# Mask chunks every three steps and more pieces of list work per step in layer 0's last dense blocks

## The chip, the core and the metric

The kernel runs on one core of a Trainium2 chip, with five engines that run side by side: PE (TensorE, matrix products), DVE (VectorE), ACT (ScalarE), POOL (GpSimd, here mostly issuing gathers) and SP (SyncE, issuing the other DMAs). The metric is the device time of one execution in microseconds, as the median of several runs; lower is better.

## What is computed

Four graph attention layers stand one behind the other over 4096 nodes with 256 features, all with one adjacency matrix. Layer 0, on which the change acts, is:

```python
h = jnp.maximum(_layernorm(x, axis=-1), 0.0)
h = h @ W.T + b_W
e = (h @ a1)[:, None] + (h @ a2)[None, :] + b_a[0]
e = jnp.where(e > 0, e, 0.2 * e)
scores = jnp.where(adjacency_matrix > 0, e, jnp.float32(NEG_INF))
attention = jax.nn.softmax(scores, axis=1)
x = x + attention @ h
```

Layers 1 to 3 have the same form with other heads and ends (layer 2 four heads, layer 3 a positive and a negative softmax). Adjacency is sparse and uneven: node i and node j are joined with a chance that falls with both numbers, so the first nodes have many neighbours and the last ones few.

## The kernel before

**Tiles.** Nodes lie in 32 tiles of 128, and eight blocks of four tiles. A target tile is done in one of two ways. Dense: the layer's first blocks (`DENSE = (4, 2, 1, 1)`, so blocks 0 to 3 in layer 0) go over all 32 source tiles, one step each; a step makes a 128x512 matrix of weights on DVE (`weigh`, L1151) and multiplies it on PE into four sums (L1193). Listed: for a target tile T of a later block, the few sources that any of its nodes have are gathered by POOL from a table in DRAM (`gather`, L532) with an index list of T, and a listed tile has 5 to 8 steps in layer 0. Four tile columns are weighed from `mpre` without a gather, then "single" gathers (s_gg), then "quad" ones of four gathers each (s_gq).

**Masks.** The adjacency matrix is loaded by SP in chunks of four source tiles by one block, in two halves (`load`, s_raw, four buffers). `mask_chunk(ib, c)` turns such a chunk into bytes on DVE (two conversions, L1472), writes it to DRAM for later layers, and notes in `seen[ib]` which sources occur (L1483). Each call also issues the next chunk's load. Dense block ib makes its own chunks as it goes, one every `CH = 4` steps; the chunks of blocks 4 to 7 are made at `sides`, one every third step, from step 2 to step 95 of the 128 dense steps. So none are left for block 3, which is steps 96 to 127.

**Lists.** When a block's eighth chunk is done, a generator `list_sources` waits for its turn (`TURNS = (4, 5, 6, 1, 7, 2, 3)`) in the queue `lists_q`. It makes the index lists of four tiles in pieces: counts (L882 to L889), a first placing (pre_p, tot_p, two matmuls, a scan L869 and an addition L878), a second placing (pre_s, tot_s, and the cast to lof), values (L928), and then per tile two one-hots of 128x1792 on DVE (L943), 28 matmuls on PE (L968, idx_ps) and the copy into an index tile (L978). A piece may give a pause in an estimated clock.

**Order.** `run(plan)` goes through the plan, which interleaves dense steps and listed steps: from dense step 48 on, one or two listed steps stand behind every dense one. At a position of the plan it fetches (makes masks, issues gathers), begins (ACT copies of gathered masks), weighs three positions later and multiplies six positions later. After each multiplied step it draws pieces from two queues: `pump(posts, rates[0])` (normalization and projection of finished tiles for layer 1, `node_rows`, with transposes s_tp, copies s_hT and products s_pj) and `pump(lists_q, rates[1])`; then up to `rates[2]` gathers of masks. A fetch that needs an index that is not there draws pieces by force. After the plan's last step what is left is drawn by force too:

```python
run(plan + listed)
push(lists_q, find_flag())
while lists_q:
    pump(lists_q, 1, force=True)
    pump(posts, 1, force=True)
```

Only then layer 1 is recorded. A scheduler puts the instructions on the engines by this order, with some freedom; POOL keeps the written order. On one engine instructions run in their order, so a waiting instruction holds all behind it. PSUM, into which PE writes, is split in six buffers for sums (`s_acc`) and two (`ps_mm`, tag "mm") that serve everything else: s_tp, s_pj, s_sT (target rows, emptied by ACT as s_grow, L1042), pre, tot and idx_ps.

Blocks 1, 2, 3 keep masks beside the rows of a layer's table. Block 7's masks (tiles 28 to 31) lie with layer 0's rows in `table_own`: a gather brings the mask too, and ACT copies it to `mlist` (L1174 for a single gather, L1084 for a quad). In layer 0 its gathers need the index of tile 28, the fifth list to be made.

Of the kernel before, what the change touches and what calls it, by code (L numbers as in the profile page):

```python
# [21 lines left out]
NT = N // P  # L22
IB = 512
NIB = N // IB
IT = IB // P
CH = 4
NCH = NT // CH
# [432 lines left out]
DENSE = (4, 2, 1, 1)  # L460
# [29 lines left out]
def list_layers(ctx: ExitStack, tc: tile.TileContext, a: dict, out: bass.AP, flag):  # L490
# [65 lines left out]
    def table_rows(t, jt):  # L556

        r0 = jt // CH * CH * P
        r0 += 1 if r0 >= HALF else 0
        return t[r0 : r0 + CH * P, :].rearrange("(p k) d -> p k d", k=CH)  # L560
# [4 lines left out]
    def mask_rows(b, jt):  # L565
        if b not in MASKS_IN:
            return table_rows(mask_t[b], jt)
        l, behind = MASKS_IN[b]
        c0 = FRONT[l] + GW[l] if behind else 0
        return table_rows(table[l], jt)[:, :, c0 : c0 + MW].bitcast(U8)  # L570
# [6 lines left out]
    def weights(l, pool, prep, q):  # L577


        L = layers[l] = Layer()  # L580
        L.l = l
        L.H, L.part = LH[l], PART[l]

        ncols = D + 3 * L.H + (D if l == 3 else 0)
        L.w = pool.tile([P, 2, ncols], F32, name=f"s_w{l}", tag=f"s_w{l}")
        L.s = small.tile([P, NT, L.H], F32, name=f"s_s{l}", tag=f"s_s{l % 2}", bufs=1)
        L.ready = [False] * NT
        L.bias = None
        L.table = table[l]
        L.made = False  # L590
        L.making = make_weights(L, pool, prep, q)
        return L
# [97 lines left out]
    def push(queue, work, delay=0.0):  # L690
        queue.append([work, clock[0] + delay])
# [14 lines left out]
    def ensure(done):  # L706
        while not done():
            assert posts
            pump(posts, 1, force=True)
# [141 lines left out]
    def list_sources(ib, seen, pool, consts):  # L851
# [75 lines left out]
        for k, block in enumerate(blocks_of):  # L927
            nc.vector.scalar_tensor_tensor(  # L928
                val[:, k, :],
                hib,  # L930
                float(block),
                code.rearrange("p t j -> p (t j)"),
                op0=ALU.is_equal,
                op1=ALU.mult,
            )
            if k % 4 == 3:
                yield
# [456 lines left out]
    with ExitStack() as phase:  # L1394
# [28 lines left out]
        L0 = weights(0, prep, prep, nc.scalar)  # L1423
# [19 lines left out]
        def load():  # L1443

            n = len(loaded)
            if n == len(order):
                return
            ib, c = order[n]
            loaded[order[n]] = []
            for h in range(2):  # L1450
                raw = stage.tile([P, half, IB], I32, name=f"s_raw_{ib}_{c}_{h}", tag="raw")
                r0 = (c * CH + h * half) * P
                nc.sync.dma_start(
                    raw,
                    a["adjT"][r0 : r0 + half * P, ib * IB : (ib + 1) * IB].rearrange(
                        "(c p) i -> p c i", p=P
                    ),
                )
                loaded[ib, c].append(raw)

        def mask_chunk(ib, c):

            load()
            if ib == 0:
                behind(c)
            m = (
                mpre[:, :, ib * IB : (ib + 1) * IB]
                if c == 0
                else mpool.tile([P, CH, IB], U8, name=f"s_m_{ib}_{c}", tag="m")
            )  # L1470
            for h, raw in enumerate(loaded[ib, c]):
                nc.vector.tensor_scalar(m[:, h * half : (h + 1) * half, :], raw, 0.0, None, op0=ALU.is_gt)  # L1472
            if ib == OWN0:
                rows_at = table_rows(table_own, c * CH)
                nc.sync.dma_start(rows_at[:, :, 0:HW].bitcast(U8), m[:, :, 0 : IB // 2])
                nc.sync.dma_start(rows_at[:, :, HW + GW[0] :].bitcast(U8), m[:, :, IB // 2 :])
            elif c > 0 or ib in MASKS_IN:
                nc.sync.dma_start(mask_rows(ib, c * CH), m)
            if ib > 0:
                if c == 0:  # L1480
                    seen[ib] = lists_p.tile([P, IT * GR, JT], BF16, name=f"seen_{ib}", tag="seen", bufs=4)
                else:
                    nc.vector.tensor_reduce(  # L1483
                        seen[ib][:, :, (c - 1) * CH : c * CH].rearrange("p a j -> p j a"),
                        m.rearrange("p j i -> p (j i)")
                        .bitcast(I32)
                        .rearrange("p (j a w) -> p j a w", j=CH, w=GP // 4),
                        AX.X,
                        ALU.max,
                    )  # L1490
                if c == NCH - 1:
                    waiting[ib] = list_sources(ib, seen[ib], lists_p, consts)
                    while turns and turns[0] in waiting:
                        push(lists_q, waiting.pop(turns.pop(0)))
            return m

        def behind(c):

            if c + 4 < NIB:
                load_x(c + 4)  # L1500
            if c == 4:
                zero_rows()
            if c == 5:
                L1 = weights(1, const, prep, nc.sync)
                L1.pre = keep.tile([P, DP, GW[1]], F32, name="pre1")
                L1.rows = rows_of(L1, rows)
                L1.pool = rows
                next(L1.making)
                push(posts, L1.making, 15.0)

        def block(ib):
            masks = {}

            def get(jt):
                if jt % CH == 0:
                    masks[jt // CH] = mask_chunk(ib, jt // CH)
                for k, at in enumerate(sides):
                    if at == ib * NT + jt:
                        mask_chunk(DENSE[0] + k // NCH, k % NCH)
                c = ib * NT + jt - sides[-1] - 1  # L1520
                if 0 <= c < NCH:
                    nc.sync.dma_start(
                        table_rows(table_own, c * CH)[:, :, HW : HW + GW[0]], L0.g[:, c * CH : (c + 1) * CH, :]
                    )
                ensure(lambda: L0.ready[jt])
                return [0], [L0.g[:, jt, :]], masks[jt // CH][:, jt % CH, :]

            return Unit(L0, ib * IT, IT, NT, get, big="growb", rates=(2, 2, 1))

        load_x(0)  # L1530
        load()
# [6 lines left out]
        for T in range(DENSE[0] * IT, NT):  # L1538
# [7 lines left out]
                rates=(1, 2, 0),  # L1546
# [3 lines left out]
        for ib in range(DENSE[0]):  # L1550
            for step in block(ib).plan():
                plan.append(step)
                if ib * NT + step[1] >= LISTED0:
                    n = 1 + step[1] % 2
                    plan += listed[:n]
                    del listed[:n]
# [23 lines left out]
    for l in (1, 2, 3):  # L1580
# [41 lines left out]
        else:  # L1622
            per = L.H
            first = []
            for ib in range(DENSE[l]):
# [6 lines left out]
                    big="o" if ib else "growb",  # L1632
                    cost=0.9 if l == 2 else 1.7,
                    per=per,
                    rates=(2, 0, 0),
# [84 lines left out]
```

## Time and profile before

| | us |
|---|---|
| median of 3 runs | 1544.14 |
| lowest, highest | 1542.4, 1545.57 |
| profiled execution, device time | 1640.54 |
| its span, first to last instruction | 1638.8 |

The profiled execution is 6% longer than a run without the profiler; all times of single instructions are of it. Its engines over the span:

```
PE 1445.7 (88%) x10558; PEld 1084.8 (66%) x10558; DVE 1182.5 (72%) x3424; ACT 497.3 (30%) x1569; POOL 1037.6 (63%) x1255
```

PEld is the load of weights into PE, beside the products. Layer 0's dense block 3 begins at about 345 us, its last dense product ends at 489.5 us, and layer 1's first transposes are at 519.2 us. "[4.60 <- X]" behind an instruction says that its engine was idle for 4.60 us before it and that X ended that.

### The profile page before, as it was taken

The page shows a single profiled execution, that of the slowest core. Times are in us where ns is not written, and L with a number is a line of the kernel's source. Part 1 is how long each engine was busy: PE and PEld are TensorE (multiplying, and loading weights), DVE is VectorE, ACT ScalarE, POOL GpSimd, SP SyncE. Part 2 cuts the span into 40 slices and gives each one's busy share as a digit, 9 for nine tenths or more (in the row PEclk, how much of TensorE's full clock was granted, in tenths as well). Part 3 has the DMA queues.
Part 4 walks back from the last instruction along what each step waited for, and adds up shares of the span by engine and source line. Part 5 has one row for each costly group of instructions (what it writes and reads, how often), then busy time and mean ns, then how long its engine had stood idle before and what let it go on. Part 6 is the DMA issues. An engine that isn't in the chain of part 4 may idle for free.

```text
span 1638.8 us, 30153 instructions
## 1 busy us (share of the span) xinstructions
PE 1445.7 (88%) x10558; PEld 1084.8 (66%) x10558; DVE 1182.5 (72%) x3424; ACT 497.3 (30%) x1569; POOL 1037.6 (63%) x1255
## 2 busy tenths in 40 slices
PE   6999898888888988888989889987877999899995
PEld 4887676666676866666645545566655877688873
DVE  6889989887677467655778879876755466577754
ACT  5631020011112023222335545565744111111111
POOL 9825888883513477767337776555556277867775
PEclk9999999999897999998999999989877999999997
DMA  7899999876414454554323333333333477766665
GB/s 261 283 320 297 320 299 293 223 201 161 115 33 145 112 152 126 141 154 133 114 73 107 97 105 97 106 90 99 91 102 106 131 217 209 217 193 198 205 184 146
DMA packets 161024, 272.72 MB, mean 166 GB/s; under 512 B 29664, under 2 KB 86462, under 8 KB 160862
## 3 DMA queue, kind: packets, MB, share of 16 engines
q1 hardware_dynamic: 117322, 146.32, 28.6%
q0 software_dynamic: 42704, 123.84, 28.2%
q8 instruction: 86, 1.41, 0.4%
q14 instruction: 76, 0.62, 0.1%
q10 hardware_dynamic: 836, 0.53, 0.1%
HBM read 225.22 MB, written 45.39 MB: 165 GB/s over the span
## 4 chain that ended last, share of the span: by engine, by line
PE 49%; DVE 7%; issue 6%; POOL 4%; DMA 4%; ACT 2%; another core or an unknown queue 1%; DVEq 0%; POOLq 0%; ACTq 0%
PE s_acc L1193 26%; PE s_pj L778 6%; PE s_acch L1210 5%; PE s_accm L1228 5%; DVE s_p L1151 3%; POOL s_gq L532 3%; PE s_acc L1130 2%; PE s_sT L1036 2%; DMA s_gq<-table,idx 1%; DMA s_gg<-table,idx 1%; PE s_acch L1130 1%; PE s_tp L746 1%; POOL s_gg L532 1%; DVE s_p L1160 1%
## 5 line engine op out<-in xcount | busy, mean ns | idle before, releaser
L532 POOL DMA_INDIRECT s_gq<-table,idx x400 | 431.8, 1080 | 188.7 <-issue 83.2
L532 POOL DMA_INDIRECT s_gg<-table,idx x258 | 277.2, 1074 | 277.4 <-DVE first L943 55.2
L1193 PE MATMUL s_acc<-g,s_p 128*128 128x257 f32 x1152 | 294.4, 401 | 17.4 <-DVE s_p L1151 12.2
L1193 PEld LDWEIGHTS s_acc<-g,s_p 128*128 128x128 f32 x1152 | 221.0, 200 | 59.7 <-DVE s_p L1151 16.5
L1193 PE MATMUL s_acc<-s_gs,s_p 128*128 128x257 f32 x896 | 212.3, 388 | 1.1 <-issue 0.9
L1151 DVE SCALAR_TENSOR_TENSOR s_p<-s_grow,pre,mpre 128x128 f32<-128x128 f32 (+1 forms) x576 | 188.4, 367 | 28.8 <-PE s_acc L1193 16.3
L778 PE MATMUL s_pj<-s_w,s_hT 128*128 128x259 f32 (+3 forms) x640 | 184.9, 428 | 24.4 <-issue 9.8
L1151 DVE SCALAR_TENSOR_TENSOR s_p<-s_grow,s_gs,s_ms 128x512 f32<-128x512 f32 x224 | 159.6, 748 | 56.5 <-PE s_acc L1193 20.1
L1193 PEld LDWEIGHTS s_acc<-s_gs,s_p 128*128 128x128 f32 x896 | 166.5, 192 | 39.0 <-issue 7.6
L1193 PE MATMUL s_acc<-pre,s_p 128*128 128x257 f32 x768 | 186.3, 391 | 3.2 <-issue 2.2
L1193 PEld LDWEIGHTS s_acc<-pre,s_p 128*128 128x128 f32 x768 | 147.2, 196 | 28.9 <-issue 4.3
L778 PEld LDWEIGHTS s_pj<-s_w,s_hT 128*128 128x128 f32 x640 | 126.2, 208 | 57.8 <-issue 14.4
L1193 PE MATMUL s_acc<-s_gg,s_p 128*128 128x257 f32 x530 | 137.9, 392 | 6.9 <-DVE s_p L1151 3.5
L1151 DVE SCALAR_TENSOR_TENSOR s_p<-s_grow,s_gg,mlist 128x128 f32<-128x128 f32 x363 | 116.5, 344 | 33.6 <-PE s_acc L1193 22.5
L541 POOL MEMSET pause<- 128x256 f32 x379 | 132.3, 349 | 0.2
L532 POOL DMA_INDIRECT mlist<-mask_t,idx x77 | 91.1, 1183 | 65.2 <-DVE idx L978 46.4
L1042 ACT ACTIVATE s_grow<-s_sT 128x256 f32<-128x256 f32 (+2 forms) x136 | 46.9, 368 | 257.4 <-PE s_sT L1036 136.5
L1107 DVE TENSOR_TENSOR s_p<-s_grow,s_gq 128x128 f32<-128x128 f32 (+1 forms) x168 | 52.4, 339 | 97.5 <-DMA s_gq<-table,idx 53.7
L1193 PEld LDWEIGHTS s_acc<-s_gg,s_p 128*128 128x128 f32 x530 | 100.2, 194 | 29.9 <-issue 8.5
L1210 PE MATMUL s_acch<-pre,s_p 128*64 128x65 f32 x1792 | 92.8, 237 | 28.9 <-issue 26.6
L1210 PEld LDWEIGHTS s_acch<-pre,s_p 128*64 128x64 f32 x1792 | 72.3, 144 | 67.0 <-issue 39.3
L1090 ACT ACTIVATE s_p<-s_grow,s_minus,pre 128x128 f32<-128x128 f32 x224 | 96.0, 485 | 62.0 <-PE s_accm L1228 25.7
(154 smaller groups left out, 2077.9 us busy)
## 6 DMA issues: line engine op xcount, KB each, us to landing
s_raw<-in_adjT SPq DMA_DIRECT2D x128, 512.0 KB
s_gs<-table SPq DMA_DIRECT2D x28, 516.0 KB
table<-s_g SPq DMA_DIRECT2D x28, 258.0 KB
mask_t<-s_m SPq DMA_DIRECT2D x28, 256.0 KB
s_ms<-mask_t SPq DMA_DIRECT2D x28, 256.0 KB
s_gq<-table,idx POOLq DMA_INDIRECT x400
table<-s_m SPq DMA_DIRECT2D x21, 256.0 KB
table<-g SPq DMA_DIRECT2D x8, 516.0 KB
```

The costliest lines, as they stand in the source:

```text
L532: nc.gpsimd.indirect_dma_start(out=dst, out_offset=None, in_=src, in_offset=bass.IndirectOffsetOnAxis(ap=index_ap, axis=0), element_offset ...
L541: nc.gpsimd.memset(pause, 0.0)
L778: nc.tensor.matmul(ps, lhsT=hT[:, c, :], rhs=L.w[:, c, k * (D + 6) : k * (D + 6) + cols], start=(c == 0), stop=(c == 1),)
L1036: nc.tensor.transpose(ps[:, h - h0, it, :], L.s[:, T0 + it, h : h + 1].to_broadcast([P, P]), ident)
L1042: nc.scalar.activation(grow[:, h1:h2, :], ps[:, h1 - h0 : h2 - h0].rearrange("p h a b -> p h (a b)"), AF.Exp, scale=scale,)
L1090: nc.scalar.activation(w[:, h, :], u.grow[:, h, :], AF.Relu, scale=g[h][:, n - 1 : n], bias=minus)
L1107: nc.vector.tensor_tensor(p4[:, h0:h1], grow[:, h0:h1], c[:, h0:h1].to_broadcast([P, h1 - h0, GR, GP]), op=op)
L1130: nc.tensor.matmul(acc, lhsT=p[:, h, part], rhs=g[:, k, h * n : (h + 1) * n - 1], start=False, stop=last, skip_group_check=True,)
L1151: nc.vector.scalar_tensor_tensor(p[:, k, :], u.grow[:, h, :], g[k][:, n - 1 : n], m, op0=ALU.min if L.l == 3 and h == 1 else ALU.max, op1= ...
L1193: nc.tensor.matmul(u.accs[it][h], lhsT=p[:, k, it * P : (it + 1) * P], rhs=g[k][:, 0:n], start=first, stop=last, skip_group_check=u.quads > 0,
L1210: nc.tensor.matmul(u.accs[0][c : c + P // 2, h, :], lhsT=p[:, h, c : c + P // 2], rhs=g[h][:, 0 : DH + 1], start=first and h == 0, stop=la ...
L1228: nc.tensor.matmul(u.accs[h], lhsT=g[k][:, 0 : DH + 1], rhs=p[:, k, :], start=first, stop=last, skip_group_check=True,)
```

## The change

In dense block 3 a chunk is made every three steps, at steps 0, 3, ..., 21, instead of every four, at steps 0, 4, ..., 28. In block 2 three pieces of list work are drawn after a dense step, and in block 3 four, instead of two; blocks 0 and 1 and the listed steps in between keep two. What is computed stays as it was.

```diff
         def block(ib):
             masks = {}
+            every = CH if ib < DENSE[0] - 1 else CH - 1
 
             def get(jt):
-                if jt % CH == 0:
-                    masks[jt // CH] = mask_chunk(ib, jt // CH)
+                if jt % every == 0 and jt // every < NCH:
+                    masks[jt // every] = mask_chunk(ib, jt // every)
...
-            return Unit(L0, ib * IT, IT, NT, get, big="growb", rates=(2, 2, 1))
+            return Unit(L0, ib * IT, IT, NT, get, big="growb", rates=(2, max(2, ib + 1), 1))
```

## The prediction

> **What bounds the kernel now.** I read in this order: the slices of the page (where PE, the matrix engine, has gaps), the table by stages for the 300 us around the change, the sums of waits there, and then PE, ACT and DVE instruction by instruction. First the stages (columns: stretch in us, its length, then busy us and count of PE, weight loads, DVE, ACT, POOL, then the granted PE clock, DMA share, GB/s).
>
> ```profile
> 240.00:345.00 105.00, 89.00 (x501) 69.35 (x499) 90.87 (x233) 14.27 (x52) 89.69 (x99) 0.97 0.92 252
> 345.00:385.00 40.00, 33.84 (x220) 26.52 (x219) 28.98 (x82) 6.64 (x24) 33.54 (x41) 0.92 0.65 160
> 385.00:414.00 29.00, 28.50 (x155) 22.92 (x156) 27.37 (x76) 4.54 (x17) 1.72 (x2) 0.94 0.61 159
> 414.00:441.90 27.90, 25.89 (x174) 21.42 (x174) 16.19 (x38) 5.13 (x19) 22.83 (x27) 0.88 0.47 117
> 441.90:461.70 19.80, 11.10 (x52) 8.38 (x50) 14.48 (x40) 2.39 (x9) 6.53 (x7) 0.89 0.40 111
> 461.70:489.40 27.70, 27.70 (x177) 23.28 (x177) 21.65 (x64) 2.53 (x10) 0.00 (x0) 0.95 0.06 20
> 489.40:519.20 29.80, 22.83 (x204) 17.66 (x202) 23.65 (x75) 9.39 (x34) 4.70 (x6) 0.71 0.38 116
> ```
>
> To 345 us POOL, DVE and DMA are all near 90%; dense block 3 then runs to 489.4 us and is held by PE, except at 441.9 to 461.7, where PE works 11.1 of 19.8 us. The last row is the drain: no dense step is left, and the rest of the lists (2 and 3) is forced out before layer 1 may begin. The two holes at 442 and 457, from the sums of waits and then from ACT and PE in order of time:
>
> ```profile
> PE tot_p L866 <- ACT s_grow L1042: 4.6, 1, 4.6
> PE pre_s L864 <- ACT s_hT L748: 4.1, 1, 4.1
> ```
> ```profile
> 446.00 0.30 ACT L1084 COPY mlist<-s_gq 128x128 uint8<-128x128 uint8 x1 [7.27 <-DMA s_gq<-table_own,idx]
> 446.21 0.27 ACT L1042 ACTIVATE s_grow<-s_sT 128x128 f32<-128x128 f32 x1
> ...
> 460.72 0.30 ACT L1084 COPY mlist<-s_gq 128x128 uint8<-128x128 uint8 x1 [4.53 <-DMA s_gq<-table_own,idx]
> 460.93 0.64 ACT L748 COPY s_hT<-s_tp 128x256 f32<-128x256 f32 x2
> ```
>
> List 2's tot_p needs one of the two ps_mm buffers; it is held by s_sT of tile 30; ACT empties it, but only behind a copy that waits for a gather from table_own. The hole at 457 is the same with s_hT and tile 31's gather. So one late gather stops PE through ACT's queue and a PSUM buffer. The drain, on DVE:
>
> ```profile
> 501.08 1.12 DVE L869 TENSOR_TENSOR_SCAN off_p<-going,tot_p 128x464 f32<-128x464 f16 x1 [2.32 <-PE tot_p L866]
> ...
> 507.42 1.08 DVE L943 TENSOR_TENSOR first<-place,lof 128x1792 f16<-128x1792 f16 x1
> 508.42 1.57 DVE L928 SCALAR_TENSOR_TENSOR val<-hib,code 128x112 f16<-128x112 f16 x8
> 509.90 2.29 DVE L943 TENSOR_TENSOR first<-place,lof 128x1792 f16<-128x1792 f16 x2
> ```
>
> From the scan at 501.08 to layer 1's first transpose at 519.22 it is one chain, list 3's own, with eight one-hots of 1.08 us at its end.
>
> **What the Trainium skill says.** "TensorE: Matmul & The Clock Gate", Architectural detail: ACT and DVE queues are strict FIFO, only PE pulls weight loads ahead; the trace agrees (s_grow ran 0.21 us after the copy that it did not need). The same page, Part 1, gives half clock to an idle PE; here the drain was granted 0.59 at 500 to 510 and 0.50 at 510 to 520 us. "Perfetto Trace Analysis", Optimizing Tensor Performance, wants matmul groups to rotate through PSUM banks so that evacuation overlaps; with two ps_mm buffers, shared by lists, transposes, projections and target rows, the 4.6 and 4.1 us show what two are worth when ACT is blocked.
>
> **The change, part by part.** The scheduler settles the order, so I counted pieces as the program is built and compared the built order on each engine.
>
> Rates. Block 2 pumps three pieces a step and block 3 four, instead of two. When the last step is recorded, 11 pieces of list 2 and 43 of list 3 are left before, and 0 and 40 after. On PE, 49 index matmuls of list 2 (of 161) leave the drain; on DVE two one-hots and the last index copies. POOL's order is identical, and from layer 1 on PE's too.
>
> (a) Drain. Before: 489.5 us (487.57 + 1.98, last dense matmul) to 519.2 = 29.7 us. After, pre_p stands on PE right behind the two transposes of tile 30/31, instead of behind those, list 2's 49 matmuls and the projections of 30, 31, 12, 13. The scan becomes DVE's limit: normalization of tiles 30/31 and the ends of 12 to 15 (about 5 us at the pitches of the before rows), scan and add 1.7, list 3 to shared with the statistics of 12 to 15 between 4.7, second placing to lof 3.0, one-hots and val 10.3 (507.42 to 517.73), last matmuls and flag 1.5: 26 us. The path gains about 4 (8 if DVE runs ahead over the first part; 0 if two PSUM buffers string it out). The projections of 14 and 15 now stand between index matmuls, so layer 1's gathers start later relative to layer 1; its first listed weight is some 28 us after its start, which covers that. −4.
>
> (b) The same 49 matmuls now stand between dense steps 25 to 30, where PE is 100% busy (27.70 of 27.70): at 0.80 us per 14 they cost 2.8. The two one-hots lie on DVE, which has 6 us free there: 0; without that cover 2.2. +2.8.
>
> (c) The two holes. Index 28, which starts the gathers of tiles 28 to 31, was ready at 414.2. The gather for tile 30 reached ACT at 446.0, 31.8 later, by POOL's pace; PE came to tot_p at 441.9, 27.7 later. After, index 28's matmuls stand a dense step earlier on PE, and list 2's placing earlier still; the first instruction that needs s_sT 30's buffer is tot_s, behind step 20 and tile 29's step 5. Counted from index 28 that is eight dense steps more than three matmuls, against six: two steps of 1.9 and three listed matmuls of 0.45, together 5.2, so PE arrives at about 33 after it, after the copy's 31.8. First hole: 4.6 to 0. Because tile 29's steps 4 and 5 now stand ahead of it, tile 31's gathers get their buffers some 2.5 us sooner, and s_hT 28 is empty at about 43 after index 28 (46.5 before); PE asks at about 42. Second hole: 4.1 to 1. That would be −7.7; the gather times are rough, so −7, bounds −8.7 and 0.
>
> (d) New waits. Index 28's second half now needs a one-hot that DVE makes only after weight 13, and PE reaches it about 1.5 us too soon. On ACT the two copies of tile 28's single gathers move ahead of s_hT 26; behind s_hT are both ps_mm buffers, so tile 30's index matmuls stop until that gather lands. It landed 6.7 us after index 28 (420.9), and PE has 6.5 us of work between: about 1 us. The trace of before does not show this wait: bounds 0 (gathers fast) and 9 (PE drawn to a stop at each). Together +2.5.
>
> Chunks. Every three steps: conversions of 0.69 and reductions of 0.69 us, same number. By weight 13 both have made chunks 1 to 4, so nothing is added to the stretch 385 to 414, where DVE is busiest (27.4 of 29). Later chunks move forward into 414 to 442, where DVE has 11.7 us free: 0, and 4 (two chunks) without it. On SP the adjacency loads of chunks 6 and 7 move ahead of the row writes of tiles 26/27, which waited until 429.0: no loss. List 3 enters its queue earlier, but stays behind list 2 almost to the end: this half alone brings about nothing.
>
> Block 2's third piece: list 6 ends earlier, in a stretch with DVE at 87%. It is work moved, not added; 0, bounds −1 and +2.
>
> Sum: −4 + 2.8 − 7 + 2.5 = −5.7 us of the profiled 1640.5. The median run is 1544.1, 0.941 of that; −5.4, so **1538.7**.
>
> **Rivals.**
> Larger gain: DVE is ahead over the end of block 3 and (d) does not happen: −6 + 2.8 − 8 + 0 = −11.2, times 0.941: 1533.6. For it: DVE has slack there. Against: two PSUM buffers.
> Holes re-form: gathers are paced by POOL and merely meet another instruction. Then (c) is −3 and the sum −4 + 2.8 − 3 + 2.5 = −1.7: 1542.5, no change.
> Slower: ACT's queue in front of list 7. With tile 28's copies ahead of s_hT 26, and the quad copy ahead of the projections of 26/27, each us by which those gathers are late is a us of PE. It decides from the point where the single gathers take over 6.5 us and the quad over 13 us from index 28 (6.7 and 13.4 in the trace). 3 us more on each makes (d) 8, and the later gathers stay late, (c) −1: −4 + 2.8 − 1 + 8 = +5.8: 1549.6. For it: four groups of gathers took 3.3 to 5.6 us to land. Against: the same chain cost PE only 1.4 us at 428.
> That the change does not do what it says: half so, since the chunk pace matters little; the pieces do move.
>
> **How the numbers follow.** Forecast 0.43, larger gain 0.16, holes re-form 0.19, slower 0.22. About 0.2%, 3.1 us, is what a measurement of this kernel tells from no change. Faster by more: 0.38 of the forecast's share and all of the larger gain, with 0.02 of the third: 0.56; slower 0.23 with a little of the third; same 0.21. The range takes (a) at −8 with the holes gone (1530) to the slower case (1549); the forecast's own is 1534 to 1542.
>
> **What would show it.** In the trace after: 112 index matmuls behind the last dense one; the drain 26 us, not 29.7; PE's waits for s_grow and s_hT near 0 and 1; a wait of idx_ps or s_tp for ACT s_hT behind mlist copies of about 1. If the drain is as long as before, (a) is wrong; if PE's idle time from 385 to the last dense matmul is not some 5 us less, (c) and (d) are.

## The result and the profile after

| | before | after |
|---|---|---|
| median, us | 1543.27 (4 runs, 1539.48 to 1545.57) | 1525.19 (4 runs, 1520.62 to 1532.37) |
| profiled execution: device time, span | 1640.54, 1638.8 | 1527.76, 1526.0 |

The ratio is 0.989 with an interval of 0.9854 to 0.9927: a gain of some 11 to 23 us where 5.4 was forecast and 13 was the edge of the range. Direction and sign were right, the size was not. Ratios and their intervals, here and below, leave out runs that took over 1.5% more than the fastest of their kernel, while differences in us are of all runs.

The two profiled executions can't be subtracted as wholes. That of before took 97 us more than its timed runs, that of after as long as its own, so it was not the profiler that made before's first trace 6% longer. From layer 1 on, where PE and POOL run the same instructions in the same order in both kernels, before's trace is 92 us longer. So I compare stretches between marks that both have. **A** runs from tile 12's target-row transposes, where dense block 3 begins, to tile 28's transpose; **B** from there to the end of the last dense product; the drain from there to layer 1's first transpose. The table by stages of after, columns as in the prediction:

```profile
336.65:384.47 47.82, 45.96 (x310) 36.83 (x309) 44.56 (x122) 11.51 (x41) 40.61 (x47) 1.00 0.76 201
384.47:472.00 87.53, 83.00 (x544) 67.63 (x545) 69.75 (x189) 10.73 (x41) 32.72 (x37) 0.94 0.37 100
472.00:498.72 26.72, 19.98 (x155) 15.10 (x153) 20.07 (x68) 9.17 (x34) 0.51 (x1) 0.73 0.39 120
```

In before's trace the three are 60.8, 91.6 and 29.7 us. PE does 544 products in B now instead of 497 and 155 in the drain instead of 203, so the index products have moved as worked out, and still B is 4.1 us shorter. The drain is 26.7 (forecast 26). A, in which the forecast changes nothing, is 13 us shorter; the experiments come back to that.

What became of the two holes of before: ACT in order of time in after, then the sums of PE's waits within its B:

```profile
428.53 0.30 ACT L1084 COPY mlist<-s_gq 128x128 uint8<-128x128 uint8 x1 [3.89 <-DMA s_gq<-table_own,idx]
428.73 0.27 ACT L1042 ACTIVATE s_grow<-s_sT 128x128 f32<-128x128 f32 x1
...
441.76 0.30 ACT L1084 COPY mlist<-s_gq 128x128 uint8<-128x128 uint8 x1 [5.46 <-DMA s_gq<-table_own,idx]
441.97 0.64 ACT L748 COPY s_hT<-s_tp 128x256 f32<-128x256 f32 x2
```
```profile
PE s_pj L778 <- ACT s_hT L748: 2.0, 1, 2.0
PE idx_ps L968 <- ACT s_g L813: 1.2, 1, 1.2
PE s_tp L746 <- ACT s_hT L748: 0.6, 1, 0.6
PE idx_ps L968 <- ACT s_hT L748: 0.5, 1, 0.5
```

s_grow still comes out 0.2 us behind the copy of tile 30's gather, but PE does not wait for it: the first hole (4.6) is gone. The second is 2.0 instead of 4.1. The last three lines, 2.3 us, are waits behind the copies of tiles 28 and 29; of these 0.5 us, s_tp for s_hT, stood in before too.

### The profile page after: what moved, and what is told of

It is laid out like the page before. It is cut to its first block, busy times and chain, and to the rows that moved or that the text cites. A ratio compares the mean times of both kernels' runs of the same rounds, so it can differ in the third digit from the quotient of the medians.

```text
span 1526.0 us, 30153 instructions
## 1 busy us (share of the span) xinstructions
PE 1387.2 (91%) x10558; PEld 1051.8 (69%) x10558; DVE 1179.9 (77%) x3424; ACT 499.9 (33%) x1569; POOL 1061.1 (70%) x1255
## 4 chain that ended last, share of the span: by engine, by line
PE 52%; DVE 18%; DMA 11%; POOL 11%; issue 5%; ACT 2%; SPq 0%; POOLq 0%; DVEq 0%; ACTq 0%
PE s_acc L1193 31%; PE s_pj L778 8%; DVE s_p L1151 7%; POOL s_gq L532 5%; DMA s_gq<-table,idx 5%; DMA s_raw<-in_adjT 4%; PE s_acch L1210 3%; PE s_accm L1228 2%; PE s_acc L1130 2%; POOL s_gg L532 2%; DVE s_p L1160 2%; PE idx_ps L968 2%; PE s_tp L746 2%; POOL pause L541 1%; DVE s_m L1472 1%
## 5 line engine op out<-in xcount | busy, mean ns | idle before, releaser
L532 POOL DMA_INDIRECT s_gq<-table,idx x400 | 444.0, 1110 | 121.9 <-issue 83.1
L532 POOL DMA_INDIRECT s_gg<-table,idx x258 | 287.7, 1115 | 229.2 <-DVE bad L1015 58.5
L1193 PEld LDWEIGHTS s_acc<-g,s_p 128*128 128x128 f32 x1152 | 219.0, 199 | 62.9 <-DVE s_p L1151 29.2
L778 PE MATMUL s_pj<-s_w,s_hT 128*128 128x259 f32 (+3 forms) x640 | 180.6, 421 | 17.5 <-ACT s_g L813 10.2
L1193 PE MATMUL s_acc<-pre,s_p 128*128 128x257 f32 x768 | 183.0, 386 | 2.3 <-DVE s_p L1151 1.5
L1151 DVE SCALAR_TENSOR_TENSOR s_p<-s_grow,s_gs,s_ms 128x512 f32<-128x512 f32 x224 | 157.7, 744 | 25.3 <-PE s_acc L1193 19.2
L1228 PE MATMUL s_accm<-s_p,s_gs 128*65 128x512 f32 x224 | 102.6, 608 | 0.9 <-DVE s_p L1151 0.9
L1472 DVE TENSOR_SCALAR s_m<-s_raw 128x1024 uint8<-128x1024 int32 x112 | 85.6, 775 | 20.9 <-DMA s_raw<-in_adjT 20.7
```

The source lines that it names most:

```text
L532: nc.gpsimd.indirect_dma_start(out=dst, out_offset=None, in_=src, in_offset=bass.IndirectOffsetOnAxis(ap=index_ap, axis=0), element_offset ...
L778: nc.tensor.matmul(ps, lhsT=hT[:, c, :], rhs=L.w[:, c, k * (D + 6) : k * (D + 6) + cols], start=(c == 0), stop=(c == 1),)
L1151: nc.vector.scalar_tensor_tensor(p[:, k, :], u.grow[:, h, :], g[k][:, n - 1 : n], m, op0=ALU.min if L.l == 3 and h == 1 else ALU.max, op1= ...
L1193: nc.tensor.matmul(u.accs[it][h], lhsT=p[:, k, it * P : (it + 1) * P], rhs=g[k][:, 0:n], start=first, stop=last, skip_group_check=u.quads > 0,
L1228: nc.tensor.matmul(u.accs[h], lhsT=g[k][:, 0 : DH + 1], rhs=p[:, k, :], start=first, stop=last, skip_group_check=True,)
```

## The experiments

Each run is timed beside the kernel before on the same chip. The runs fell on several chips, and on most of them every kernel takes some 8% longer (before: 1651 to 1676 us; 1543 and 1546 on two occasions), so times are compared within a row only. "Difference" is the mean of all runs of the kernel less that of before, with one standard error; "ratio" is to before, with its 95% interval. A, B, drain and the two waits are from the run's trace; "hole 1" is PE's wait for s_grow at list 2's tot_p, "hole 2" its wait for s_hT behind tile 31's quad gather.

| run | median / before | difference | ratio | A | B | drain | hole 1 | hole 2 |
|---|---|---|---|---|---|---|---|---|
| before, four traces | | | | 60.8 to 62.8 | 90.3 to 92.0 | 29.7 to 30.9 | 3.3 to 4.6 | 4.0 to 4.1 |
| before_second (one of the four) | 1670.6 / 1671.8 | −4.5 ± 3.1 | 0.9955 (0.9906 to 1.0003) | 61.9 | 90.3 | 29.8 | 4.0 | 4.0 |
| after, first | 1525.2 / 1543.3 | −17.1 ± 3.0 | 0.989 (0.9854 to 0.9927) | 47.8 | 87.5 | 26.7 | 0 | 2.0 |
| after_second | 1653.7 / 1671.8 | −19.3 ± 4.8 | 0.9872 (0.9803 to 0.994) | 74.4 | 87.7 | 26.7 | 0 | 1.9 |
| after_third | 1635.2 / 1651.2 | −13.2 ± 3.5 | 0.9897 (0.9854 to 0.9941) | 50.7 | 85.8 | 26.6 | 0 | 1.9 |
| rates_only | 1673.5 / 1675.4 | +0.3 ± 4.5 | 1.0103 (1.004 to 1.0166) | 50.2 | 93.5 | 27.6 | 0 | 4.9 |
| rates_second | 1676.5 / 1676.0 | −0.1 ± 3.9 | 0.9955 (0.9899 to 1.001) | 64.8 | 92.6 | 27.3 | 0 | 5.0 |
| pace_only | 1673.4 / 1675.4 | −0.3 ± 3.2 | 1.0035 (0.9998 to 1.0071) | 64.3 | 90.4 | 29.7 | 3.8 | 3.6 |
| pace_second | 1672.8 / 1676.0 | −2.5 ± 2.3 | 1.001 (0.9975 to 1.0045) | 59.9 | 90.9 | 29.7 | 5.3 | 3.7 |
| block3_only | 1673.1 / 1675.4 | +3.7 ± 4.5 | 1.0116 (1.0045 to 1.0188) | 63.5 | 92.4 | 26.4 | 0 | 4.9 |
| block3_second | 1677.8 / 1676.0 | +2.9 ± 2.4 | 1.0049 (1.0006 to 1.0092) | 62.7 | 93.4 | 27.7 | 0 | 4.9 |
| block2_only | 1664.3 / 1671.8 | −8.6 ± 3.1 | 0.9907 (0.9875 to 0.9939) | 72.3 | 89.8 | 29.7 | 2.5 | 4.0 |
| block2_second | 1670.8 / 1676.0 | −5.2 ± 2.8 | 0.9968 (0.9932 to 1.0003) | 60.4 | 91.4 | 29.7 | 2.2 | 4.0 |
| direct_before | 1640.7 / 1651.2 | −9.9 ± 3.0 | 0.993 (0.9899 to 0.9962) | 64.3 | 85.1 | 30.6 | 0 | 0 |
| direct_after | 1629.9 / 1651.2 | −19.2 ± 2.9 | 0.9872 (0.9835 to 0.9909) | 56.4 | 83.3 | 27.6 | 0 | 0 |
| direct_rates | 1520.7 / 1546.3 | −28.5 ± 1.7 | 0.9815 (0.979 to 0.9841) | 53.9 | 77.7 | 26.3 | 0 | 0 |
| direct_after_second | 1518.7 / 1546.3 | −29.2 ± 2.0 | 0.9808 (0.9782 to 0.9834) | 53.0 | 80.4 | 27.2 | 0 | 0 |
| rate8 | 1643.2 / 1651.2 | −7.0 ± 2.9 | 0.9924 (0.9892 to 0.9956) | 73.4 | 93.3 | 25.3 | 0 | 3.3 |

before_second is the kernel before under another label: its −4.5 shows what the same code can differ by. B, the drain and the holes of one kernel agree from chip to chip within 2 us (B with direct_after's edit, 83.3 and 80.4, excepted); A does not.

### The parts alone

rates_only is the change without its pace, pace_only the pace without the rates, block3_only and block2_only one rate each:

```diff
-            every = CH if ib < DENSE[0] - 1 else CH - 1
+            every = CH
```
```diff
-            return Unit(..., rates=(2, max(2, ib + 1), 1))
+            return Unit(..., rates=(2, 2, 1))
```
```diff
-            return Unit(..., rates=(2, max(2, ib + 1), 1))
+            return Unit(..., rates=(2, 3 if ib == 2 else 2, 1))
```

The first is rates_only, the second pace_only, the third with the first block2_only; block3_only has 4 in block 3 and 2 elsewhere. Expected of the first timings:

> Chunks every four steps again, three and four pieces in blocks 2 and 3. Theory A (the rates do it, the pace of the chunks nothing): all of the gain, 14 to 20 us under the kernel before. Theory C (the pace matters: adjacency loads no longer stand behind row writes on SP, conversions move to where DVE has room): 4 to 9 us under it.

> Chunks every three steps, two pieces everywhere. Theory A: within 3 us of the kernel before. Theory C: 8 us or more under it.

> Chunks every four steps, four pieces in block 3, two in block 2. Theory A with all of it in block 3: as rates_only, within 3 us. If the third piece in block 2 matters (list 6 ends earlier, so its masks and list 1 too): half of rates_only's gain or less.

> The kernel before with three pieces a step in block 2 alone (block 3 stays at two, chunks every four steps). S: stretch A falls to 47 to 51, the rest as before (tile 28 to the last dense product 90 to 93, drain 29 to 31), time 10 to 13 us below before. T: A as in before, time within 2 us of before (as predicted: work moved, nothing saved).

The pace alone: nothing, as forecast, and drain and holes stay. But the rates alone bring nothing either, which neither theory had expected. They do much of what the forecast asked of them: list 2 leaves the drain, which falls to 27.6, and the first hole goes. Yet B grows to 93.5 instead of falling to 87. ACT of rates_only, then PE:

```profile
421.34 0.65 ACT L748 COPY s_hT<-s_tp 128x256 f32<-128x256 f32 x2 [3.48 <-remote]
...
460.02 0.30 ACT L1084 COPY mlist<-s_gq 128x128 uint8<-128x128 uint8 x1 [5.14 <-DMA s_gq<-table_own,idx]
460.22 0.64 ACT L748 COPY s_hT<-s_tp 128x256 f32<-128x256 f32 x2
```
```profile
421.76 0.95 PE L968 MATMUL idx_ps<-val,first 128*128 128x6 f16 x14 [2.21 <-ACT s_hT L748]
...
460.64 2.09 PE L778 MATMUL s_pj<-s_w,s_hT 128*128 128x259 f32 x4 [4.95 <-ACT s_hT L748]
```

The wait of 2.21 us, in front of tile 30's index products, is not a gather's: the s_hT that ends it had itself waited for 3.48 us after the last copy ahead of it was done, in a wait of the kind described below for stretch A. The second hole is 4.95 us here, larger than before. Counted from the copy of index 28, PE comes to these projections after some 43.4 us in both traces with the rates alone and after 43.4, 43.9 and 43.7 in the three of after: the same. Tile 31's quad gather is copied by ACT after 47.8 and 47.8 us with the rates alone, after 44.8, 45.1 and 44.9 with rates and pace. So beside the rates the pace makes the gather 3 us earlier, not PE later.

In this pair of traces the hole costs more than its 5 us. The groups of PE from there to the last dense product, of rates_only and then of after_third (busy us, mean ns of one, idle before):

```profile
L1193 PE MATMUL s_acc<-g,s_p 128*128 128x257 f32 x82 | 21.9, 412 | 0.0
...
L778 PE MATMUL s_pj<-s_w,s_hT 128*128 128x259 f32 x8 | 3.6, 594 | 4.9 <-ACT s_hT L748 4.9
```
```profile
L1193 PE MATMUL s_acc<-g,s_p 128*128 128x257 f32 x74 | 18.3, 388 | 0.0
...
L778 PE MATMUL s_pj<-s_w,s_hT 128*128 128x259 f32 x8 | 2.0, 394 | 1.9 <-ACT s_hT L748 1.9
```

After 4.9 us of idling a projection takes 594 ns, after 1.9 us 394; the granted clock of that tail is 0.91 against 1.00. With one dense step more in it (82 products against 74), the tail is 32.7 against 27.9 us. The contrast is not as clean in the other traces: 466 to 554 ns after 4.9 to 5.0 us, but also 454 and 529 after 1.9 and 2.0.

A second set on one chip, to see whether the time follows the traces:

> Both rates, chunks every four steps as before. If the pace brings nothing (as predicted), this is the whole gain: 12 to 18 us below before, drain 26 to 28, stretch from tile 28 to the last dense product 86 to 94. If the rest of the gain needs the pace, 3 to 8 us below.

> Chunks every three steps in block 3, rates as before. Predicted: nothing, within 3 us of before, drain 29 to 31, stretch from tile 28 to the last dense product 90 to 92. Rival (the pace brings the rest): 6 to 12 us below.

> Four pieces in block 3 alone. By the prediction this holds the drain (-3) and most of what the last stretch of block 3 gives: 3 to 8 us below before. If the rest of the gain is block 2's third piece, no more than that; if block 3's rate brings all, 12 to 18 below.

> Three pieces in block 2 alone. Predicted 0 (-1 to +2). The first timing of it was 7.5 us below before: 5 to 10 below if that is a gain of its own, within 3 if it was noise; drain 29 to 31 and the stretch from tile 28 to the last dense product 90 to 92 in both cases.

It does, in part. Rates alone and block 3's rate alone bring no gain again (by the ratios block 3's rate is even slower by 0.5 to 1.2%): most of the drain's 3 us is given back in B (rates +1.9 and −2.6 against the means of before, 91.2 and 30.0). The pace has no gain of its own. Block 2's third piece alone seems to have one, −8.6 and −5.2, though B and drain hardly move. It is not certain: the second ratio's interval reaches 1, and the first set of runs is the one in which before_second, the same code, came out at −4.5. The three outcomes add up to some −5, and the change as a whole has −13 to −19: pace and rates are worth more together than apart.

### Before and after again: stretch A

A second trace of before, before_again, had been expected to come back to some 1543 us if the first was no exception; it took 1683.1, with A 62.8 and both holes there (3.7 and 4.1 us).

> The kernel before once more, to see its trace and its times in the same conditions as the runs below. Stretch A is the time from tile 12's target-row transposes (start of dense block 3) to tile 28's; it was 60.8, 62.8 us in the two traces of before, 64.3 with the pace alone, 63.5 with block 3's rate alone, but 47.8 in after and 50.2 with both rates. Theory S (block 2's third piece shortens A by 12 us): A is 60 to 64 again. Theory T (A was long because engines stopped there for want of instructions, by chance; waits whose end is put down to 'remote' or 'issue'): A is 49 to 52 in a trace that has few such waits, and anything from 49 to 65 in one that has many.

> The changed kernel once more. Both theories: from last dense product to layer 1's first transpose 26 to 28 us, waits for s_grow and s_hT at list 2 and tile 31 of 0 and up to 3. S: stretch A 47 to 51 whatever the other waits are; ratio to before 0.986 to 0.992. T: A long as well if this trace has many 'remote' and 'issue' waits; ratio 0.994 to 0.998 (the 6 us of the prediction).

> The kernel before, one look. Without the waits that no event ends: stretch A 48 to 54, tile 28 to the last dense product 90 to 92 with waits for s_grow and s_hT of 3.5 to 5, drain 29 to 30, time near 1543. With them: A 60 to 64 and time 1640 or more, as in the three traces so far; the last two stretches the same in both cases.

The theory that block 2's piece by itself shortens A by 12 us fell in these runs: A was 74.4 in after_second and 72.3 in block2_only. Nor did the other theory's "within 2 us" for block2_only hold (−8.6 ± 3.1). What fills A is shown by DVE, ACT and PE of before_second in order of time:

```profile
379.06 0.60 DVE L1151 SCALAR_TENSOR_TENSOR s_p<-s_grow,s_gg,mlist 128x128 f32<-128x128 f32 x2
393.70 0.17 DVE L978 TENSOR_SCALAR idx<-idx_ps 128x10 int32<-128x10 f32 x1 [14.03 <-remote]
```
```profile
390.80 0.26 ACT L800 ACTIVATE s_g<-s_pj,s_r 128x2 f32<-128x2 f32 x1 [11.30 <-remote]
```
```profile
384.72 0.53 PE L968 MATMUL idx_ps<-val,first 128*128 128x10 f16 x7
385.11 1.11 PE L1193 MATMUL s_acc<-g,s_p 128*128 128x257 f32 x4
393.92 2.10 PE L778 MATMUL s_pj<-s_w,s_hT 128*128 128x259 f32 x4 [7.70 <-DVE idx L978]
```

The profile puts the end of the index products that L978 reads at 385.25, but it models the ends of products. DVE takes them at 393.70, and as no product ends there, the profile names nobody ("remote"). The changes of semaphores that the trace keeps do tell: L978 waits for the semaphore that PE raises, and this one changes at 393.67 and 393.72. For ACT's s_g it changes at 390.78, where the profile has the product end at 384.88. So DVE and ACT wait for a signal from PE, which comes 8.4 and 5.9 us behind the modelled ends. Whether the product or only its signal is late stays open.

In each trace of 1630 us and more, of before and of the changed kernel alike, DVE and ACT together have 21 to 36 waits of over 1 us that are put down to "remote". They are 473 in these seventeen traces, and 470 of them end within 0.15 us of a change of PE's semaphore. In the three traces of some 1520 us (the first of after, direct_rates, direct_after_second) there is none, and A is 47.8, 53.9 and 53.0. At the instruction shown, DVE is idle for 9.7 us in the first trace of before, 11.3 in pace_only and 11.1 in direct_before; in after_second, block2_only and rate8 it is another one, a one-hot with ACT's s_grow beside it (7.6 and 21.2 us in after_second).

So the first comparison set a trace with these waits against one without, and its 13 us in A can't be put down to the change. That none of them is the change's is not shown either. The nine traces without block 2's third piece all have an A of 59.9 us or more; of the eleven with it, six have 47.8 to 56.4, three of these among the short executions, in which no kernel without the piece was traced. before_third, run for that, has the waits again (A 61.4).

### ACT's queue taken away

In direct_before, direct_after and direct_rates a DMA from SP makes the eleven copies of tiles 28 to 31's gathered masks, and a quad's weights are masked straight from the gathered tile, so they no longer wait for a copy either (the two effects were not separated); lists, pieces and gathers stay as in before, after and rates_only.

```diff
-            if (u.L.l, u.T0, i) in quad_masks:
+            if u.L.l and (u.L.l, u.T0, i) in quad_masks:
...
-            nc.vector.tensor_tensor(
-                p[:, 0:own, :], p[:, 0:own, :], m.unsqueeze(1).to_broadcast([P, own, P]), op=ALU.mult
-            )
+            q, k = p[:, 0:own, :], m.unsqueeze(1).to_broadcast([P, own, P])
+            if (L.l, u.T0, i) in quad_masks: q, k = p4[:, 0:own], quad_masks[L.l, u.T0, i][1].unsqueeze(1).to_broadcast([P, own, GR, GP])
+            nc.vector.tensor_tensor(q, q, k, op=ALU.mult)
...
-            if (L.l, u.T0, i) in copies:
-                nc.scalar.copy(*copies.pop((L.l, u.T0, i)))
+            for d in (copies, quad_masks):
+                if (L.l, u.T0, i) in d: (nc.scalar.copy if L.l else nc.sync.dma_start)(*d.pop((L.l, u.T0, i)))
```

> The kernel before, with the eleven copies of gathered masks of tiles 28 to 31 (mlist) taken off ACT: a DMA from SP makes them, and the quad's weights are masked straight from the gathered tile. The two holes of before (PE waiting 4.6 us for s_grow and 4.1 us for s_hT) should be gone if ACT's queue behind a late gather makes them: the stretch from tile 28's transpose to the last dense product falls from 90.3 to 92.0 (three traces) to 83 to 86 us, the drain stays 29.7. Rival (the gathers' pace itself holds PE, whatever ACT does): the stretch stays 89 to 92, the waits only change their names to s_gq or s_p.

> The same edit in the changed kernel. Of the holes only 2.9 us are left there, and the new waits for s_hT behind tile 28's copies are some 2 us: the stretch from tile 28's transpose to the last dense product falls from 87.6 to 83 to 86, the drain stays 26.7. If it falls by nothing, the new waits (d) of the prediction were not ACT's queue.

> Both rates, chunks every four steps, and the copies of tiles 28 to 31's gathered masks made by a DMA from SP instead of ACT. If the pace matters only through ACT's queue behind late gathers: the stretch from tile 28 to the last dense product falls from 92.6 and 93.5 (rates alone) to 83 to 86, as in direct_after, drain 27 to 28, time 8 to 20 us below before. If the pace matters in another way (chunks on DVE, adjacency loads, the clock): the stretch stays above 89 and the time within 5 us of before.

All three as expected if ACT's queue makes the holes. In direct_before both are gone and B is 85.1 instead of 91.2; a wait of 3.2 for s_r takes a part of their place. In direct_rates the sums of PE's waits within B have two lines left:

```profile
PE s_sT L1036 <- DVE off_s L869: 0.4, 1, 0.4
PE s_sT L1036 <- DVE off_p L869: 0.3, 1, 0.3
```
```profile
391.27:468.99 77.72, 77.29 (x544) 65.21 (x545) 68.75 (x189) 8.06 (x30) 31.05 (x34) 1.00 0.42 115
468.99:495.27 26.28, 19.46 (x155) 14.77 (x152) 19.87 (x68) 9.01 (x34) 0.00 (x0) 0.75 0.38 122
```

PE works 77.3 of 77.7 us at a granted clock of 1.00, with the 544 products that B has in after. B (77.7) and the time (−28.5) even fall further than expected (83 to 86; 8 to 20), and so do direct_after_second's 80.4 and −29.2 (82 to 85; 14 to 24). And direct_rates, without the pace, is level with direct_after_second beside it (1520.7 and 1518.7), where rates_only was far from after: this fits a pace that helps the rates through ACT's queue. It is no full proof, since these two ran on the chip with the shorter times, where the rates with ACT's copies were not run, and the same kernel's gain is larger there (direct_after −19.2 ± 2.9, direct_after_second −29.2 ± 2.0). Their ratios to before, 0.9815 and 0.9808, lie below all three of the changed kernel, which was not run beside them. On the chip where direct_after ran beside it the difference of the two, −6.1 ± 4.2 us, is not certain; in B it is −2.5.

### More pieces still

rate8 draws eight pieces in block 3 instead of four.

> The changed kernel with eight pieces a step in block 3 instead of four. Of list 3, 30 pieces are left behind the last dense step instead of 40: both placings and the first one-hot move in. If the drain is list 3's own chain on DVE, it falls from 26.7 to 17 to 21 us, and the stretch before it grows by at most 2; time 5 to 9 us below the changed kernel. If two PSUM buffers and the projections of the last tiles make the drain, it stays at 24 to 27.

The forecast drain of 17 to 21 did not come: 25.3, with B at 93.3, and the time is 6.2 ± 4.2 us above after_third's beside it instead of 5 to 9 below. The scans and products of both placings did move ahead of it, but the second placing's cast to lof (506.69) and all eight one-hots still run behind the last dense product, as in after. DVE in the drain, then PE:

```profile
512.49 1.09 DVE L943 TENSOR_TENSOR first<-place,lof 128x1792 f16<-128x1792 f16 x1 [1.63 <-PE idx_ps L968]
...
529.91 0.17 DVE L978 TENSOR_SCALAR idx<-idx_ps 128x7 int32<-128x7 f32 x1 [4.38 <-PE idx_ps L968]
```
```profile
524.61 3.66 PE L778 MATMUL s_pj<-s_w,s_hT 128*128 128x259 f32 x8
528.06 1.81 PE L968 MATMUL idx_ps<-val,first 128*128 128x7 f16 x28
```

The one-hots now wait for PE, which serves the last projections between the index products, at a granted clock of 0.60 (0.71 in after_third's drain), and the last index copy waits 4.38 us for it: in this trace the end of the drain is PE's, not DVE's. The 10 pieces more in block 3 meanwhile made a new wait of 6.2 us for s_hT in B.

## Why the prediction was wrong in size

**(a) Drain, −4.** Right: 30.0 (four traces) to 26.7 (three), 112 index products behind the last dense step. The working gave 26.

**(b) Products moved into block 3, +2.8.** B has 47 more, as counted; no run prices them alone. PE's busy time in B is 80.1 to 82.3 us in the traces of before and 80.3 to 83.0 in those of after.

**(c) Holes, −7.** Right for the first: 4.6 to 0, and the copy of tile 30's gather comes 31.6 us after index 28 (31.8 in the forecast). The second was forecast at 1 and is 2.0, 1.9, 1.9.

**(d) New waits, +2.5.** 2.3 us in the first trace, 3.5 and 3.6 in the other two, at the named places; 0.5 of it was there before. With (c) and (d) PE's idle time in B falls from 10.3 to 5.2 us on average, about as forecast.

Together B and drain fall from 121.2 to 113.7 us, −7.5, where the sum had −5.7. So the steps that the sum priced came out near their forecast, and the rival of the slower case, ACT's queue in front of list 7, was not what the change does. The miss lies in the two terms that were put at 0.

**Block 2's third piece, 0, bounds −1 and +2: the step on which the size failed, as far as is known.** The change as a whole brings some −16 us (three timings, −13 to −19), and B and drain hold 7.5 of them. The other 8.5 lie outside these two stretches, where the prediction has only this piece and the pace, which alone brings nothing. Alone this piece measured −8.6 ± 3.1 and −5.2 ± 2.8 on two chips, on the good side of the bounds, with the doubt that before_second's −4.5 leaves. I took "work moved, not added" for no gain. The time is measured, its place isn't: the stretches where it should lie are the ones with the waits for PE's signal. That the two amounts are the same is not shown, and plain addition does not bear it out: the rates alone have this piece too, with B and drain at 120.5 us, hardly less than before's 121.2, and gain nothing. The cause of these 8.5 us stays open.

**Chunks, 0: the step of the mechanism that failed.** "This half alone brings about nothing" held. That "the chunk pace matters little" to the change did not: with the pace the whole has −13 to −19 us, without it +0.3 ± 4.5 and −0.1 ± 3.9. The error was to price the pace by busy time on DVE and by loads on SP, next to the old order, and then to leave it out of the sum for the new one. With the rates in place, tile 31's gather comes 3 us earlier with the pace; without it the second hole is 5 us, and B and drain are 120.5 us instead of 113.7. My working of (c) and (d) had been done on the order with both halves, so its numbers were those of the pair, and the text credits them to the rates; for the same reason this step is not what made the sum too small. B and drain show 6.8 us of the pace's worth, the times some 16: the rest is as open as above, and rates and pace alone were timed only on the chips with the longer times. What makes the gather earlier in detail (tile 30's index is copied 18.6 us after tile 28's with the rates alone and 11.1 to 12.5 with both, but 10.1 with block 3's rate alone, whose gather is late as well) is not settled.

**The conversion.** Scaling the profiled sum by 0.941 took before's trace for an execution slowed evenly. B and drain of after are the same in a trace of 1526 us and in one of 1660 us (together 114.3 and 114.5); the extra time of before's trace sits elsewhere. The factor did little harm here (−5.7 to −5.4), but it was not right.

## What to carry to other kernels

Where a late transfer reaches the critical engine through another engine's queue, take the waiting instruction out of that queue: that was worth 10 us in the kernel before, and the pace no longer mattered then. It did not make the change needless: on one chip direct_after is 9.4 ± 3.7 us below direct_before. Two halves of a change that both move the same schedule can't be priced one at a time on the old schedule: work out each half alone and the pair. And before two traces are compared, run the old kernel a second time: stretches that repeat (here B and drain, within 2 us) carry an argument, and those that don't carry none.

## What the runs showed of the hardware

In each of seventeen executions of 1630 us and more, DVE and ACT together waited 21 to 36 times for over 1 us for a signal from PE that no modelled end of a product accounts for. It came far behind that end: 8.4 us for L978 of before_second, where POOL went on issuing gathers, and 12.8 for ACT's s_grow of after_second (idle for 21.2). In three executions of some 1520 us there was no such wait, with the same instructions or nearly so. The Trainium skill, "Runtime: NRT & Kernel Launch", Instruction fetch mechanics, tells of instructions that come in blocks by DMA, which would be a candidate for a halt; in before_second the instruction queues show a packet at 364, 369 and 380 us and none from 381 to 400, so the wait that ended at 393.70 did not end with one. Why the signal is late is open.

The clock answers to small idle times unevenly: after 1.9 us the next eight projections ran at 394 ns on average in one execution and 454 in another, after 2.0 us at 529, and after 4.9 to 5.0 us at 466 to 594 in four. Nor is a half clock a sign of an idle PE alone, as the prediction took it for the drain: at 510 to 520 us of before's first trace the granted clock is 0.50 while PE is busy for 9.0 of the 10 us.
